# Layer 3 of a four-layer graph network: H3's three parts multiplied as one 384-column product, the decoder in written order

## The chip, the cores and the metric

The kernel runs on one core of one Trainium2 chip. The time is the device time of one execution in microseconds (us). Before the change 14 runs gave a median of 3338.72 us, with 3335.47 the lowest and 3339.78 the highest.

The core has engines that run side by side and wait for each other by semaphores: PE (matrix products, whose weight loads the profile lists as PEld), DVE (the vector engine), ACT (activation functions), POOL and SP. SP, ACT and POOL also start DMA transfers; the time that an engine's instruction queue spends on that is listed under SPq, ACTq and POOLq. Each engine runs its own instructions in order.

## What is computed

The reference takes 3125 nodes with 256 features and 100000 weighted edges through four graph layers. Each is added to its input and normalised per node. The change is in the last one. Cut to what matters (3125 nodes, 256 features in, 128 and 64 hidden):

```python
h = x @ W_conv                                # 256 -> 128
out = segment_sum(h[row] * (dis[row] * dis[col])[:, None], col) + b_conv
h = relu(out)
z = h @ W_lin + b_lin                         # 128 -> 64
d = relu(z @ W_dec1 + b_dec1)                 # 64 -> 128
out = d @ W_dec2 + b_dec2                     # 128 -> 256
x = layernorm(x + out)                        # the result
```

`dis` is one over the root of a node's degree, its own loop included. The sum over edges is a product with the (sparse) matrix of edge counts.

## The kernel before, in words

Nodes lie in 25 blocks of 128 (`NBK = 25`, `P = 128`). The matrix of edge counts is kept dense as 25 slabs, one for each block of targets: a slab is 128 x 25 x 128 numbers in bf16, 800 KB. Layer 0 builds the slabs and stores them in DRAM (`slabs`); layer 3 loads them again. `load_slab(b)` (line 728) takes one of the four buffers named `wo` and starts the load on SP (line 730). Layers 1 and 2 use the same four buffers.

The features that layer 3 sums are scaled by `dinv` and split into three bf16 parts whose sum is the f32 value. They lie in `H3`, a tile of shape [128, 25, 3, 128]: node in the block, block, part, feature. The last lines of layer 2's loop fill it, block by block (lines 1052 to 1055; the split is lines 637 to 643). So the 25th block of `H3` is there only when layer 2's last block is done.

In layer 3 the three parts are summed by `apply_parts` (line 698): for each of the 25 source blocks and each of three parts, one matmul with the slab's 128 x 128 block as weights and 128 columns of `H3`, line 702, all into one accumulator. That is 75 matmuls of 128 columns for each target block. (Layers 0 and 1 use the same line with 256 columns.)

The loop at line 1081 then does for each block b:

- line 1084, DVE: accumulator times `dinv` plus `b_conv`, into the tile `tmp`;
- line 1086, PE: transpose; line 1088, ACT: relu into `dec`;
- line 1090, PE: product with `W_lin`; line 1091, ACT: plus `b_lin`;
- line 1093, PE: product with `W_dec1`; line 1094, ACT: relu of that plus `b_dec1`;
- line 1095, PE, in the helper `product` (line 620): product with `W_dec2`, 256 columns;
- lines 1096 and 1097, DVE: added to `x2`, and `b_dec2` added;
- `norm` (line 627): DVE 629, 630, 632, ACT 633 (a square root), DVE 634 and 635;
- `write` (line 1066): four DMAs of 32 KB to the output, two started on SP and two on ACT (line 1071; block 0 uses lines 1076 and 1079).

The matmuls of lines 1086, 1090, 1093 and 620 are in f32, those of line 702 in bf16. The accumulators come from a pool `psA` of two, the results of 1090, 1093 and 620 from a pool `psM` of one.

A planner orders the instructions of each engine ahead of time, from priorities and its own costs, and may move them across the blocks of this loop and into the end of layer 2. The order that it chose is the one in the trace. Only the first stage of the kernel is inside `tc.manual_schedule` (line 500), under which the engines named get their instructions in the order in which the program writes them.

Of the kernel before, what the change touches and what calls it, by code (L numbers as in the profile page):

```python
# [8 lines left out]
F32 = mybir.dt.float32  # L9
BF = mybir.dt.bfloat16  # L10
I32 = mybir.dt.int32
AF = mybir.ActivationFunctionType
OP = mybir.AluOpType
AX = mybir.AxisListType
# [4 lines left out]
P = 128  # L19
# [12 lines left out]
def column(vec):  # L32
    return vec.rearrange("(n o) -> n o", o=1)
# [4 lines left out]
NBK = 25  # L38
# [61 lines left out]
def dense_path(ctx: ExitStack, tc: tile.TileContext, a: dict, out: bass.AP, flag: bass.AP):  # L100
    nc = tc.nc
# [22 lines left out]
    dinv = top.tile([P, NBK], F32, name="dinv")  # L124
# [7 lines left out]
    def halves(v):  # L132
        return [v[:, k * P:(k + 1) * P] for k in range(D // P)]
# [5 lines left out]
    with ExitStack() as st:  # L139
# [131 lines left out]
        for k in range(KD):  # L271
            nc.tensor.matmul(vps, attn[:, k:k + 1].to_broadcast([P, P]), we[:, k, :],
                             start=(k == 0), stop=(k == KD - 1), skip_group_check=True)
        for k in range(KD):
            nc.tensor.matmul(kps, attn[:, k:k + 1].to_broadcast([P, P]), be[:, k:k + 1],
                             start=(k == 0), stop=(k == KD - 1), skip_group_check=True)
        nc.scalar.activation(kc, kps, AF.Copy)
        for i, n in ((1, "edge_weight"), (2, "edge_weight_n2")):
            w = two.tile([P, EC], F32, name="w", bufs=1)
# [294 lines left out]
    psM = ctx.enter_context(tc.tile_pool(name="d_psM", bufs=1, space=PSUM))  # L574
    psB = ctx.enter_context(tc.tile_pool(name="d_psB", bufs=3, space=PSUM))
    psA = ctx.enter_context(tc.tile_pool(name="d_psA", bufs=2, space=PSUM))
# [25 lines left out]
    def bias(pool, v, name):  # L602
        t = pool.tile([P, v.shape[0]], F32, name=name)
        nc.scalar.dma_start(t, row_bcast(v))
        return t
# [17 lines left out]
    def project(v, w, m):  # L623
        t = transposed(halves(v))
        return product([t[:, k, :] for k in range(KD)], [w[:, k, :] for k in range(KD)], m)
# [21 lines left out]
    def halfslab(name, bufs=2, cols=P):  # L647
        t = oh.tile([P, HALF[0] * TB, P], BF, name=name, tag=name, bufs=bufs)
        return t if cols == P else t.rearrange("p t (h c) -> p (t h) c", c=cols)
# [48 lines left out]
    def apply_parts(slab, parts, m):  # L698
        p = psA.tile([P, 512], F32, name="acc")
        for s in range(NBK):  # L700
            for k in range(3):
                nc.tensor.matmul(p[:, :m], slab[:, s, :], parts[:, s, k, :m],  # L702
                                 start=(s == 0 and k == 0), stop=(s == NBK - 1 and k == 2))
        return p[:, :m]

    def apply_f32(slab, H, m):
        p = psA.tile([P, 512], F32, name="acc")
        for (o, n), t in zip(half_slabs(), slab):
            for s in range(n):
                nc.tensor.matmul(p[:, :m], t[:, s, :], H[:, o + s, :m], start=(o + s == 0), stop=(o + s == NBK - 1))  # L710
        return p[:, :m]

    def weighted_slab(pool, b, ks, kd, w3, turned=False):

        slab = []
        for o, n in half_slabs():
            os = onehot(cut(ks, b, o, n), n * TB, "os")
            od = onehot(cut(kd, b, o, n), n * TB, "od", HP)
            wo = weighted(od, [w3[:, k, o * TB:(o + n) * TB, :] for k in range(3)], n * TB)
            t = pool.tile([P, HALF[0], P], F32, name="slab_f", bufs=3)  # L720
            if turned:
                build_turned(t, n, wo, os)
            else:
                build_slab(t, b, o, n, os, wo)
            slab.append(t)
        return slab

    def load_slab(b):
        s = halfslab("wo", 4)[:, :NBK, :]
        nc.sync.dma_start(s, slabs[b].rearrange("p (s d) -> p s d", d=P))  # L730
        return s
# [20 lines left out]
    with tc.tile_pool(name="layer0", bufs=1) as pool:  # L752
        W2 = weight(pool, a["L0_gnn_W2"], "W2")
        H1 = pool.tile([P, NBK, 3, D], BF, name="H1")
        for b in range(NBK):
            load_records(b)
            slab = halfslab("wo", 4)[:, :NBK, :]
# [5 lines left out]
            p = apply_parts(slab, H0, D)  # L763
            y = wk.tile([P, D], F32, name="tmp")
            nc.scalar.activation(y, p, AF.Relu, scale=dinv[:, b:b + 1])
            p = project(y, W2, D)
# [7 lines left out]
        for j in range(TB):  # L774
            for d in range(0, NBK, 5):
                p = psT.tile([P, P], BF, name="tp")
                nc.tensor.transpose(p[:5 * NBK, :], by_tile[:, j, d * NBK:(d + 5) * NBK, 0], ident_b)
                y = pool.tile([P, P], BF, name="rowt", bufs=2)
# [27 lines left out]
        for b in range(NBK):  # L806
            p = apply_parts(load_slab(b), H1, D)
# [4 lines left out]
            p = project(x[:, b, :], WnT, D)  # L812
            nc.vector.tensor_add(H[:, b, :D], p, bn)
            m = wk.tile([P, D], F32, name="tmp")
# [25 lines left out]
    def slab_weights(b, field, by_target):  # L840

        r = wk.tile([P, TS, 4], F32, name="rec_b", bufs=3)
        v = trows if by_target else slot_rows.rearrange("(p d s j) w -> p d s (j w)", p=P, d=NBK, s=NBK)
        if by_target:
            nc.sync.dma_start(r, v[:, b * TS:(b + 1) * TS, :])
        else:
            nc.sync.dma_start(r.rearrange("p (d j) w -> p d (j w)", j=TB), v[:, :, b, :])
        w3 = wk.tile([P, 3, TS, 2], BF, name="w3")
        weights_split(w3, wk, r[:, :, field], TS, 2)
        return w3  # L850


    with tc.tile_pool(name="layer1", bufs=2) as pool:
# [39 lines left out]
        for b in range(NBK):  # L893
            w3 = wk.tile([P, 3, TS, 2], BF, name="w3")
            weights_split(w3, wk, q[:, b * TS:(b + 1) * TS], TS, 2)
            slab = weighted_slab(pool, b, keys, keyd, w3)
            p = apply_f32(slab, H, D + 1)
# [3 lines left out]
            y = wk.tile([P, D], F32, name="tmp")  # L901
# [12 lines left out]
    F0, F1 = a["L3_gnn_W_lin"].shape  # L914
    H3 = late.tile([P, NBK, 3, F0], BF, name="H3")
    with tc.tile_pool(name="layer2", bufs=1) as pool:
# [25 lines left out]
        def aggregate(b, ks, kd, w3, X, turned=False):  # L942
            return apply_f32(weighted_slab(pool, b, ks, kd, w3, turned), X, D + 1)

        with tc.tile_pool(name="layer2a", bufs=1) as pa:
# [73 lines left out]
            for b in range(NBK):  # L1019
                p = aggregate(b, keys, keyd, slab_weights(b, 1, True), x1[:, :, 1:])  # L1020
                y = pa.tile([P, D + 1], F32, name="sums", bufs=2)
# [4 lines left out]
        with tc.tile_pool(name="layer2c", bufs=1) as pb:  # L1026
            for b in range(NBK):
                p = aggregate(b, keys_t, keyd_t, slab_weights(b, 2, False), x1, True)

                y = pb.tile([P, 2 * (D + 1)], F32, name="both_in", bufs=2)  # L1030
                nc.sync.dma_start(y[:, :D + 1], a_in[:, b, :])
                nc.scalar.activation(y[:, D + 1:], p, AF.Copy)
                t = transposed(halves(y[:, :D]) + halves(y[:, D + 2:]) + halves(x[:, b, :]))
                p = psT.tile([P, 4, P], F32, name="tp")
# [3 lines left out]
                w = [m[:, k, :] for m in W_x + [W_h2h] for k in range(KD)]  # L1038
                p = product([t[:, k, :] for k in range(3 * KD)] + [r], w + [u], G)
# [3 lines left out]
                y = pb.tile([P, G], F32, name="gate")  # L1043
# [8 lines left out]
                p = project(x2[:, b, :], W_conv, F0)  # L1052
# [5 lines left out]
    with tc.tile_pool(name="layer3", bufs=1) as pool:  # L1058
        b_conv, b_dec2 = bias(pool, a["L3_gnn_b_conv"], "b_conv"), bias(pool, a["L3_gnn_b_dec2"], "b_dec2")
        w = {}  # L1060
        for n in ("W_lin", "W_dec1", "W_dec2", "b_lin", "b_dec1"):
            v = a["L3_gnn_" + n]
            v = v if n[0] == "W" else column(v)
            w[n] = pool.tile(list(v.shape), F32, name=n)
            nc.scalar.dma_start(w[n], v)
        def write(b):
            for c, p0 in enumerate((0, HP, HP + 1, 1)):
                q = (nc.sync, nc.scalar)[c % 2]
                if b:
                    n0 = FEW + NG * c + (b - 1, NG - b)[c % 2]  # L1070
                    q.dma_start(out[n0:n0 + 4 * NG * (HP // 2 - 1) + 1:4 * NG, :], x2[p0:p0 + HP - 1:2, b, :])  # L1071
                    continue
                r = range(c, FEW_ROWS, 4)
                first = c < FEW
                if first:
                    q.dma_start(out[c:c + 1, :], x2[p0:p0 + 1, b, :])
                m = len(r) - first
                n0 = P * NG + r[first]
                q.dma_start(out[n0:n0 + 4 * (m - 1) + 1:4, :], x2[p0 + 2 * first:p0 + 2 * (first + m) - 1:2, b, :])

        for b in range(NBK):
            p = apply_parts(load_slab(b), H3, F0)
            y = wk.tile([P, D], F32, name="tmp")
            nc.vector.scalar_tensor_tensor(y[:, :F0], p, dinv[:, b:b + 1], b_conv, op0=OP.mult, op1=OP.add)
            p = psT.tile([P, 4, P], F32, name="tp")
            nc.tensor.transpose(p[:, 0, :], y[:, :F0], ident)
            t = pool.tile([P, 3, P], F32, name="dec", bufs=3)
            nc.scalar.activation(t[:, 0, :], p[:, 0, :], AF.Relu)
            p = psM.tile([P, 512], F32, name="mm")
            nc.tensor.matmul(p[:F1, :P], w["W_lin"], t[:, 0, :], start=True, stop=True)  # L1090
            nc.scalar.activation(t[:F1, 1, :], p[:F1, :P], AF.Identity, bias=w["b_lin"])
            p = psM.tile([P, 512], F32, name="mm")
            nc.tensor.matmul(p[:, :P], w["W_dec1"], t[:F1, 1, :], start=True, stop=True)
            nc.scalar.activation(t[:, 2, :], p[:, :P], AF.Relu, bias=w["b_dec1"])
            p = product([t[:, 2, :]], [w["W_dec2"]], D)
            nc.vector.tensor_add(x2[:, b, :], x2[:, b, :], p)
            nc.vector.tensor_add(x2[:, b, :], x2[:, b, :], b_dec2)
            norm(b, x2)
            write(b)

# [620 lines left out]
```

## Time and profile before

The profiled execution took 3336.9 us, with a span of 3335.1 us on its core; the rest lies outside the span. It is 1.8 us under the median of the 14 runs.

| | PE | PEld | DVE | ACT | POOL |
|---|---|---|---|---|---|
| busy in the whole span, us | 2719.6 | 2100.8 | 2121.4 | 927.3 | 795.1 |
| share of the span | 82% | 63% | 64% | 28% | 24% |
| busy from 3151 to 3322 us, us | 149.9 | 123.4 | 61.3 | 29.7 | 0.0 |

Layer 3 is the last 180 us or so. Its first line 1084 starts at 3152.5 us, its last at 3319.9, and the span ends at 3335.1. In between blocks follow each other every 7.03 us. A timeline gives, for each line, the start in us, the duration in us, the engine, the line of the kernel, the operation, what is written and read, and in brackets the idle time of the engine just before, with what ended it. Neighbouring instructions of one kind are merged ("x55"). A matmul's listed duration runs to the end of its result; the next matmul can start earlier. A windows table gives, for a stretch, its length, the time for which each engine was busy in it (with the number of instructions) and the granted PE clock, 1.00 being full speed.

### The profile page before, as it was taken

Reading aid. Unit: us, or ns where it says so; the run is one execution under the profiler, and the core shown is the slowest. Engines: PE = TensorE matmul, PEld = TensorE weight load, DVE = VectorE, ACT = ScalarE, POOL = GpSimd, SP = SyncE. Lnnn points to the kernel's source line nnn. Section 1 sums busy time; section 2 is a strip of 40 time slices with the busy share of each in tenths; the row PEclk is TensorE's granted clock in tenths of the full one; section 3 lists DMA queues with packets and bytes.
Section 4 is the critical chain, followed back from the end, with each engine's and each line's share of the span. In section 5 each row is a group of like instructions: output and inputs, shape, how many; then the busy total and the mean of one; then the engine's idle time right before and its main releaser. Section 6 shows DMA issues by size and latency. Waiting matters only on the chain.

```text
span 3335.1 us, 66141 instructions
## 1 busy us (share of the span) xinstructions
PE 2719.6 (82%) x28824; PEld 2100.8 (63%) x28824; DVE 2121.4 (64%) x3844; ACT 927.3 (28%) x1844; POOL 795.1 (24%) x879
## 2 busy tenths in 40 slices
PE   4466654555541999999899999999999999999987
PEld 2234432333221888788688888888887676676676
DVE  8999964555542655355588888667666566566333
ACT  2222222222220444200122222222223343343311
POOL 4677777777775000000000000000000000000000
PEclk7556555555555999999899999999999999999999
DMA  4122222222212211556300000100011101100242
GB/s 146 52 65 79 79 67 69 70 69 70 77 30 77 88 70 80 194 215 228 129 2 2 2 2 14 36 16 16 16 14 16 12 10 10 12 10 7 75 133 88
DMA packets 169936, 203.86 MB, mean 61 GB/s; under 512 B 117592, under 2 KB 142669, under 8 KB 163363
## 3 DMA queue, kind: packets, MB, share of 16 engines
q1 hardware_dynamic: 130955, 186.94, 17.2%
q10 hardware_dynamic: 13592, 10.94, 1.1%
q0 software_dynamic: 25088, 1.66, 0.7%
q8 instruction: 227, 3.72, 0.5%
q14 instruction: 74, 0.61, 0.1%
HBM read 167.60 MB, written 31.86 MB: 60 GB/s over the span
## 4 chain that ended last, share of the span: by engine, by line
PE 47%; POOL 20%; DVE 17%; issue 8%; ACT 4%; DMA 2%; ACTq 1%; POOLq 0%; DVEq 0%; SPq 0%
POOL table L473 19%; PE acc L710 17%; PE acc L702 12%; PE mm L620 7%; PE slab L682 5%; DVE wo L836 4%; DVE os L656 3%; PE tp L613 2%; PE slab L694 1%; PE look L798 1%; ACT xT L614 1%; DVE st L629 1%; DVE od L656 1%; DMA rec_b<-table 1%; ACTq L1071 1%
## 5 line engine op out<-in xcount | busy, mean ns | idle before, releaser
L473 POOL DMA_INDIRECT table<-rec,row x784 | 755.5, 964 | 275.9 <-issue 228.9
L710 PE MATMUL acc<-x,slab_f 128*128 128x257 f32 x2500 | 592.6, 386 | 0.0
L836 DVE TENSOR_TENSOR wo<-od,w 128x1664 bf16<-128x1664 bf16 (+1 forms) x450 | 434.3, 984 | 132.0 <-PE slab L682 108.2
L702 PEld LDWEIGHTS <-wo 128*128 128x128 bf16 x5625 | 476.0, 99 | 61.9 <-issue 10.7
L710 PEld LDWEIGHTS acc<-x,slab_f 128*128 128x128 f32 x2500 | 455.9, 189 | 71.4 <-issue 5.7
L682 PEld LDWEIGHTS <-os 128*128 128x128 bf16 x8750 | 297.5, 99 | 116.6 <-issue 91.9
L702 PE MATMUL acc<-H,wo 128*128 128x256 bf16 (+1 forms) x3750 | 342.5, 247 | 1.2 <-ACT H L639 0.8
L656 DVE TENSOR_TENSOR os<-iota_b,keys 128x3328 bf16<-128x3328 bf16 (+1 forms) x150 | 272.8, 1818 | 111.1 <-PE slab L682 110.0
L391 PEld LDWEIGHTS <-ohd 128*52 128x52 bf16 x784 | 106.6, 159 | 338.3 <-issue 299.8
L710 PE MATMUL acc<-features,slab_f 128*128 128x257 f32 x1250 | 297.3, 388 | 0.0
L682 PE MATMUL slab<-wo,os 128*128 128x64 bf16 x7500 | 261.1, 193 | 13.6 <-ACT slab_f L683 8.4
L710 PEld LDWEIGHTS acc<-features,slab_f 128*128 128x128 f32 x1250 | 227.9, 190 | 43.3 <-issue 12.1
L388 PE MATMUL cnt<-pre,ident_b 52*52 52x442 bf16 x48 | 25.1, 523 | 276.6 <-ACT pre L398 276.6
L683 ACT ACTIVATE slab_f<-slab 128x512 f32<-128x512 f32 (+1 forms) x350 | 182.6, 549 | 145.9 <-PE slab L682 140.8
L702 PE MATMUL acc<-features,wo 128*128 128x256 bf16 x1875 | 212.7, 273 | 0.0
L965 POOL COPY keys_t<-keys 128x2500 bf16<-128x2500 bf16 x1 | 2.5, 2522 | 721.6 <-ACT tmp L902 721.6
L319 DVE TENSOR_TENSOR aside<-aside,features 128x256 f32<-128x256 f32 x25 | 10.8, 432 | 223.9 <-ACT features L316 223.9
L391 PE MATMUL cnt<-oh,ohd 128*52 128x416 bf16 (+15 forms) x784 | 152.1, 383 | 1.3 <-DVE ohd L331 1.3
L485 ACT ACTIVATE tick<-gap 1x1 f32<-1x1 f32 x47 | 7.4, 158 | 516.6 <-POOL tock L486 378.1
L656 DVE TENSOR_TENSOR od<-iota_b,keyd 128x1664 bf16<-128x1664 bf16 (+1 forms) x150 | 147.5, 983 | 0.0
L437 DVE TENSOR_SCALAR eq<-gap 128x512 bf16<-128x512 f32 x196 | 121.8, 680 | 29.4 <-ACT tick L485 29.2
L1044 DVE TENSOR_TENSOR gate<-mm,bx 128x512 f32<-128x512 f32 x25 | 17.3, 692 | 190.9 <-PE mm L620 190.9
(293 smaller groups left out, 3701.9 us busy)
## 6 DMA issues: line engine op xcount, KB each, us to landing
ea<-in_edge_attr SPq DMA_DIRECT2D x49, 1024.0 KB
wo<-slabs SPq DMA_DIRECT2D x50, 800.0 KB
os<-rows SPq DMA_DIRECT2D x25, 832.0 KB
slabs<-wo SPq DMA_DIRECT2D x25, 800.0 KB
od<-rows SPq DMA_DIRECT2D x25, 768.0 KB
table<-rec,row POOLq DMA_INDIRECT x784
dr<-db_row SPq DMA_DIRECT2D x49, 208.0 KB
rec_b<-table SPq DMA_DIRECT2D x75, 100.0 KB
```

The costliest lines, as they stand in the source:

```text
L391: nc.tensor.matmul(cnt[:, c + 1:, :], it["by_target"][:, c], it["by_source"][:, c:c + 1, :].to_broadcast([P, CH - c, KB]), start=False, st ...
L437: nc.vector.tensor_scalar(eq[:, 4 * g:4 * g + 4, :], gap, 0.0, None, op0=OP.is_equal)
L473: i = nc.gpsimd.indirect_dma_start(out=table, out_offset=bass.IndirectOffsetOnAxis(ap=ready[k][:, c:c + 1], axis=0), in_=rec[:, k * CH + c ...
L613: nc.tensor.transpose(p[:, j, :], srcs[i + j], ident)
L614: nc.scalar.activation(t[:, i:i + n, :], p[:, :n, :], AF.Copy)
L620: nc.tensor.matmul(p[:, :m], l, r, start=(i == 0), stop=(i == len(w) - 1))
L656: nc.vector.tensor_tensor(in_pairs(t[:, :n, :]), repeat(iota_b[:, :cols], n), pair(k, cols), op=OP.is_equal)
L682: nc.tensor.matmul(p[:, i - g, own], l, r, start=(m == 0), stop=(m == len(terms) - 1))
L683: nc.scalar.activation(dst[:, g:g + w, :], p[:, :w, :], AF.Copy)
L702: nc.tensor.matmul(p[:, :m], slab[:, s, :], parts[:, s, k, :m], start=(s == 0 and k == 0), stop=(s == NBK - 1 and k == 2))
L710: nc.tensor.matmul(p[:, :m], t[:, s, :], H[:, o + s, :m], start=(o + s == 0), stop=(o + s == NBK - 1))
L836: nc.vector.tensor_tensor(in_pairs(t[:, :n, :]), in_pairs(oh[:, :n, :]), pair(w3[k], HP), op=OP.mult)
```

## The change

`apply_parts` is no longer used by layer 3. For each block b and each source block s there is one matmul of 384 columns (`H3[:, s]` with parts and features side by side) in place of three of 128; the accumulator holds the three partial sums side by side. A new DVE instruction adds the three (`tensor_reduce` over a view in which the parts are innermost, 128 x 384 in, 128 x 128 out, into the unused half of the tile `tmp`), and line 1084's operation then reads that half.

The 25 matmuls of a block are cut into five pieces of five. The decoder of a block is cut into five steps, and the steps of block b-1 stand between the pieces of block b: step, piece, step, piece and so on. The results of the `W_lin` and `W_dec1` products move from the pool `psM` to the pool `psB` (three buffers, tag `slab`). Slabs are loaded three blocks ahead, and the whole is written inside `tc.manual_schedule` for PE, DVE, ACT and SP.

```diff
-        for b in range(NBK):
-            p = apply_parts(load_slab(b), H3, F0)
+        slab, acc = {}, {}
+
+        def piece(b, i):
+            for s in range(5 * i, 5 * i + 5):
+                nc.tensor.matmul(acc[b][:, :3 * F0], slab[b][:, s, :], H3[:, s].rearrange("p k m -> p (k m)"),
+                                 start=(s == 0), stop=(s == NBK - 1))
+
+        def decode(b):
             y = wk.tile([P, D], F32, name="tmp")
-            nc.vector.scalar_tensor_tensor(y[:, :F0], p, dinv[:, b:b + 1], b_conv, op0=OP.mult, op1=OP.add)
+            nc.vector.tensor_reduce(y[:, F0:], acc.pop(b)[:, :3 * F0].rearrange("p (k m) -> p m k", k=3), axis=AX.X, op=OP.add)
+            nc.vector.scalar_tensor_tensor(y[:, :F0], y[:, F0:], dinv[:, b:b + 1], b_conv, op0=OP.mult, op1=OP.add)
+            yield
             p = psT.tile([P, 4, P], F32, name="tp")
             nc.tensor.transpose(p[:, 0, :], y[:, :F0], ident)
             t = pool.tile([P, 3, P], F32, name="dec", bufs=3)
             nc.scalar.activation(t[:, 0, :], p[:, 0, :], AF.Relu)
-            p = psM.tile([P, 512], F32, name="mm")
-            nc.tensor.matmul(p[:F1, :P], w["W_lin"], t[:, 0, :], start=True, stop=True)
-            nc.scalar.activation(t[:F1, 1, :], p[:F1, :P], AF.Identity, bias=w["b_lin"])
-            p = psM.tile([P, 512], F32, name="mm")
-            nc.tensor.matmul(p[:, :P], w["W_dec1"], t[:F1, 1, :], start=True, stop=True)
-            nc.scalar.activation(t[:, 2, :], p[:, :P], AF.Relu, bias=w["b_dec1"])
+            yield
+            p = psB.tile([P, 4, P], F32, name="slab")
+            nc.tensor.matmul(p[:F1, 0, :], w["W_lin"], t[:, 0, :], start=True, stop=True)
+            nc.scalar.activation(t[:F1, 1, :], p[:F1, 0, :], AF.Identity, bias=w["b_lin"])
+            yield
+            p = psB.tile([P, 4, P], F32, name="slab")
+            nc.tensor.matmul(p[:, 0, :], w["W_dec1"], t[:F1, 1, :], start=True, stop=True)
+            nc.scalar.activation(t[:, 2, :], p[:, 0, :], AF.Relu, bias=w["b_dec1"])
+            yield
             p = product([t[:, 2, :]], [w["W_dec2"]], D)
             nc.vector.tensor_add(x2[:, b, :], x2[:, b, :], p)
             nc.vector.tensor_add(x2[:, b, :], x2[:, b, :], b_dec2)
             norm(b, x2)
             write(b)
 
+        with tc.manual_schedule(engines={e.engine for e in (nc.tensor, nc.vector, nc.scalar, nc.sync)}):
+            for b in range(3):
+                slab[b] = load_slab(b)
+            for b in range(NBK + 1):
+                steps = decode(b - 1) if b else iter(())
+                if b < NBK:
+                    acc[b] = psA.tile([P, 512], F32, name="acc")
+                if b + 3 < NBK:
+                    slab[b + 3] = load_slab(b + 3)
+                for i in range(5):
+                    next(steps, None)
+                    if b < NBK:
+                        piece(b, i)
```

## The prediction, made before the changed kernel was run

> **What bounds the kernel now.** The page comes first: its span, and the rows of the 40 slices for PE and the PE clock.
>
> ```profile
> span 3335.1 us, 66141 instructions
> PE   4466654555541999999899999999999999999987
> PEclk7556555555555999999899999999999999999999
> ```
>
> Layer 3 fills the last two slices. PE looks full there, but busy shares are averages, so next comes the timeline of one block from the middle of layer 3, cut to what matters.
>
> ```profile
> 3190.39 0.42 DVE L1096 TENSOR_TENSOR features<-features,mm 128x256 f32<-128x256 f32 x1 [4.14 <-PE mm L620]
> ...
> 3192.60 0.41 DVE L635 TENSOR_SCALAR features<-features,stats,rstd 128x256 f32<-128x256 f32 x1
> 3193.01 0.35 DVE L1084 SCALAR_TENSOR_TENSOR tmp<-acc,dinv,b_conv 128x128 f32<-128x128 f32 x1
> ...
> 3193.05 1.38 ACTq L1071 DMA_DIRECT2D out<-features  x2
> ...
> 3193.42 0.33 PE L1086 MATMUL tp<-ident,tmp 128*128 128x128 f32 x1
> ...
> 3193.58 0.50 PE L702 MATMUL acc<-H,wo 128*128 128x128 bf16 x6
> ...
> 3194.53 0.28 ACT L1088 ACTIVATE dec<-tp 128x128 f32<-128x128 f32 x1 [2.15 <-PE acc L702]
> ...
> 3194.86 0.43 PE L1090 MATMUL mm<-dec,W_lin 128*64 128x128 f32 x2 [0.77 <-ACT dec L1088]
> ...
> 3195.74 0.48 PE L1093 MATMUL mm<-dec,W_dec 64*128 64x128 f32 x2
> ...
> 3196.68 0.70 PE L620 MATMUL mm<-W_dec,dec 128*128 128x256 f32 x2
> ...
> 3197.22 3.23 PE L702 MATMUL acc<-H,wo 128*128 128x128 bf16 x55
> 3197.42 0.42 DVE L1096 TENSOR_TENSOR features<-features,mm 128x256 f32<-128x256 f32 x1 [4.06 <-PE mm L620]
> ```
>
> Read it as a ring. From line 1096 to the end of 635, DVE normalises block b: 2.62 us. Straight behind that, with no idle time, it starts line 1084 of block b+1 (0.35), then PE transposes. ACT can't take the transposed block (1088) before 4.14 after 1096, since its queue is busy for 1.38 us with the two output DMAs of block b, which wait for 635. Then W_lin at 4.47, W_dec1 at 5.35, W_dec2 at 6.29, and line 1096 of block b+1 at 7.03. So a chain through DVE, ACT and PE sets the pace, not PE's amount of work. The planner fits the 75 sums into its gaps: 6, 7, 7 and 55, the 55 beside the normalisation; PE idles only 0.77 us a block.
>
> The last view is the granted clock. It changes at 3153.02, 3159.85 and 3323.70: distances of 6.83 and 163.85 us, 2 and 48 times 3.41. So I cut windows of 3.41 us that end where the clock fell (first, second, third and fifth; the fourth and sixth are those where it stayed).
>
> ```profile
> 3149.61:3153.02 3.41, 1.66 (x11) 1.06 (x12) 1.12 (x4) 1.06 (x4) 0.00 (x0) 1.00 0.00 0
> 3320.28:3323.70 3.42, 1.36 (x6) 0.73 (x7) 0.00 (x0) 1.01 (x3) 0.00 (x0) 1.00 0.16 38
> 1074.30:1077.70 3.40, 1.19 (x22) 1.00 (x20) 0.00 (x0) 0.00 (x0) 0.00 (x0) 1.00 0.84 194
> 1371.30:1374.70 3.40, 2.30 (x21) 1.96 (x19) 1.59 (x6) 0.48 (x2) 0.00 (x0) 1.00 0.75 243
> 1374.70:1378.10 3.40, 0.98 (x8) 0.64 (x7) 0.00 (x0) 0.28 (x1) 0.00 (x0) 1.00 0.95 384
> 3187.00:3190.40 3.40, 2.58 (x24) 1.88 (x25) 0.01 (x1) 1.01 (x3) 0.00 (x0) 1.00 0.74 216
> ```
>
> The second number is PE's busy time. With 49% or less the clock fell to 0.50; with 67 and 76% it held.
>
> **The change, part by part.** Times count from line 1096 of block b-1.
>
> *Sums.* 55 matmuls of 128 columns in 3.23 us are (3.23 - 0.22)/54 = 55.7 ns apart. For 256 columns, layer 1 has 50 in 5.62 us, (5.62 - 0.27)/49 = 109.2. One step of 128 costs 53.5, so 384 columns cost 162.7 ns (bounds: 109, and three times 55.7 = 167). A block needs 4.07 us in place of 4.18: 0.11 less, on an engine that doesn't set the pace. A piece of five is 0.81. What matters is where pieces stand. In written order each is in PE's queue ahead of the next step.
>
> *Added reduce.* 128x384 from PSUM. The SBUF row of line 816 (256 in, 0.42 us) and the PSUM row of 801 (150 in, 0.31) give 0.155 + 1.04 ns an element: 0.56. Bounds: 0.42 (as 816), and 0.83 if the stride costs what it does in line 560, 784 strided elements in 1.53 us, 1.75 ns each. I take 0.56, as PSUM row 801 is nearest. In written order it stands behind the normalisation of block b-1 on DVE (`write` and `norm` end step five, the reduce opens the next block): 2.62 to 3.18. Line 1084's operation then runs 3.21 to 3.56 (0.35 kept; its operand is now in SBUF), transpose at 3.62 against 3.03.
>
> *ACT.* The two output DMAs keep their place; ACT is free at 4.14 as before. The transposed block is there at 4.0. So of the 0.59 that the reduce adds, ACT's queue hides nearly all: W_lin could start at 4.47 still. SP's queue has each load written before the writes of the block before; a load waits for a buffer freed an iteration ago and a write for 635, so a later load is held one block at most, and each is issued three blocks (23 us) ahead, when a whole block moves 928 KB in 7.03 us at a DMA share of 0.45: nothing. The `psB` move costs nothing: three free buffers and no builder left.
>
> *Pieces in the chain.* After the transpose (PE takes 0.16 until the next matmul starts: 3193.42 to 3193.58) a piece runs 3.78 to 4.60, so W_lin starts at 4.60. It occupies 0.36 (start to start), W_dec1 0.42, W_dec2 0.54. Now W_lin to W_dec1 is 0.36 + 0.82 = 1.18 against 0.88 before, W_dec1 to W_dec2 0.42 + 0.81 = 1.23 against 0.94. W_dec1 at 5.78, W_dec2 at 7.01, and line 1096 after 0.74 more: **7.75 us a block against 7.03**. Lower bound with the cheap reduce: 7.62; upper: 8.02.
>
> *What goes late.* PE has pieces until 1.43 after 1096 (the last of a block and the first of the next, from -0.20 on), then nothing until the transpose at 3.62: a stall of 2.19 us in every block, where before 47 sums stood. A 3.41 us window that holds it whole has 1.22 busy, 36%: the clock falls. Going by 49%, any window with 1.74 us of the stall falls. Each block slides against the windows, and walking through it (7.75 us is 2.27 windows, 9.4 is 2.75) a window falls in some 15 of 24 blocks. For 3.41 us PE then runs at half speed, in the part of the block that is all PE, so about 1.7 us of work is late; less what lies in the stall, 1.65. After line 1084's start at 3152.5 the clock stayed low for two windows, 6.83 us, which would cost 3.3; other rises (1067.5, 1384.9) took one dense window. I take one, as the pieces are dense.
>
> Here a page speaks against me. The Trainium skill, "TensorE: Matmul & The Clock Gate", section "Why this matters for your kernels", asks only for no idle gaps over some 3 us between bursts. By it 2.19 us would be harmless, and the sum below would lose its clock term and be 3360. This trace disagrees: in the window that ends at 3153.02 no single gap exceeds 1 us, and the clock fell.
>
> *Head and tail.* Before, the ends of layer 2 hid the sums of two blocks, and line 1096 ran 3158.17 to 3317.29 for blocks 0 to 23: 159.1 us, 2.6 under 23 rings. In written order only block 0 can run ahead. New: 23 x 7.75 = 178.3, **+19.2**. The head: block 0's last matmul still waits for H3's last part (3152.18), the reduce adds 0.56 and the clock is low there as before: +1.3 by 1096 of block 0. If block 0's 24 matmuls (3.9 us) can't start before layer 2's last product at 3150.4, another 2.1; I take half, **+2.3** in all. The last block (7.49 from 1096 to 1096) has no pieces, but waits for ACT as before: 4.14 + 3.35 = 7.49: 0. The end after 1096 stays.
>
> *Sum.* 19.2 + 2.3 + 15 x 1.65 = 46. The profiled execution took 3336.9, giving 3383; the median is 1.8 higher: **3385**.
>
> **Rivals.**
> *No clock drops.* The bracket of 49 to 67% counts listed durations, and short f32 products may count less than dense pieces do. Then 3338.7 + 21.5 = 3360. For: steady blocks before held 1.00 throughout; against: the four falls.
> *Long drops.* Two windows each: 21.5 + 15 x 3.3 = 71, 3410. For: 3153 to 3159.85, in this very decoder; against: other rises.
> *Faster.* If the order written lets reduce, 1084's operation and 1088 of the next block stand ahead of `norm` and `write`, PE sets the pace: 5 x 0.81 + 0.16 + 0.36 + 0.42 + 0.54 = 5.55 us, 23 x 5.55 = 128, 31 less: with the head 3310. For: the decoder then hides wholly behind pieces; against: the diff writes `norm` first, and ACT's DMAs too. It decides from a ring under 6.9 us, 0.85 off DVE's and ACT's part alike.
> *The change does next to nothing.* If pieces cost less in the chain than worked out (0.59 of the 0.72) and the clock holds, a ring of about 7.1: 3338.7 + 4 + 2 = 3345.
>
> **How the numbers follow.** Clock drops of one window 0.57 (3368 to 3402: 10 to 20 blocks, reduce and head bounds), no drops 0.20 (3352 to 3367), long drops 0.10, faster 0.08, next to nothing 0.05. The range 3352 to 3408 holds the first two and some of the long drops, 0.8. Within 0.2% (6.7 us, about what this kernel's runs can tell): the last, 0.05. Slower 0.87, faster 0.08.
>
> **What would show it.** In the changed trace: line 620's helper to the next line 1096 unchanged at 0.74; between 1096 and the next, 7.7 us where the clock is 1.00 and about 9.4 where it falls; PE idle 2.2 us before the transpose, ended by DVE; a reduce of 0.56; five-matmul runs of 0.81 plus latency; a granted clock of about 0.8 over layer 3, with steps 3.41 us apart. I am wrong if DVE runs the reduce ahead of line 629, if the stall is under 1.2 us, or if the clock stays at 1.00.

## The result and the profile after

The changed kernel takes 3376.9 us, median of 6 runs (3375.25 to 3378.63), against 3338.54 before (28 runs). That is 38.4 us more, a ratio of 1.0116 with a 95% interval of 1.0106 to 1.0126. The profiled execution took 3377.3 us with a span of 3375.5.

The line that adds the product with `W_dec2` (1096 before, 1109 now) is a good clock for the stage. From its first to its last start layer 3 took 166.6 us before (3158.17 to 3324.78) and takes 205.2 us now (3159.99 to 3365.22): 38.6 of the 40.4 us between the two profiled executions; the other 1.8 us lie ahead of it. Below, "layer 3" means this stretch.

First the page of the changed kernel: the span, and the slices of PE and of the PE clock.

```profile
span 3375.5 us, 63667 instructions
PE   4467645545532999999799999999999999999776
PEclk7555655555556999999899999999999999999888
```

The last three slices hold layer 3. PE is at 7, 7 and 6 tenths where it was at 8 and 7, and its clock at 8. Next the timeline of two neighbouring blocks: start, duration, engine, line, operation, what is written and read, and the idle time just before with what ended it.

```profile
3249.63 0.55 DVE L1092 TENSOR_REDUCE tmp<-acc 128x128 f32<-128x384 f32 x1
3249.74 1.38 ACTq L1071 DMA_DIRECT2D out<-features  x2
3250.22 0.35 DVE L1093 SCALAR_TENSOR_TENSOR tmp<-tmp,dinv,b_conv 128x128 f32<-128x128 f32 x1
...
3250.62 0.33 PE L1096 MATMUL tp<-ident,tmp 128*128 128x128 f32 x1 [1.95 <-DVE tmp L1093]
...
3251.22 0.28 ACT L1098 ACTIVATE dec<-tp 128x128 f32<-128x128 f32 x1 [2.15 <-PE tp L1096]
...
3251.69 0.43 PE L1101 MATMUL slab<-dec,W_lin 128*64 128x128 f32 x2
...
3252.97 0.48 PE L1105 MATMUL slab<-dec,W_dec 64*128 64x128 f32 x2
...
3254.21 0.59 PE L620 MATMUL mm<-W_dec,dec 128*128 128x256 f32 x2
...
3254.84 0.42 DVE L1109 TENSOR_TENSOR features<-features,mm 128x256 f32<-128x256 f32 x1 [4.28 <-PE mm L620]
...
3257.06 0.41 DVE L635 TENSOR_SCALAR features<-features,stats,rstd 128x256 f32<-128x256 f32 x1
...
3258.38 0.33 PE L1096 MATMUL tp<-ident,tmp 128*128 128x128 f32 x1 [1.95 <-DVE tmp L1093]
...
3259.45 0.44 PE L1101 MATMUL slab<-dec,W_lin 128*64 128x128 f32 x2
...
3261.53 0.79 PE L1105 MATMUL slab<-dec,W_dec 64*128 64x128 f32 x2
...
3263.51 0.59 PE L620 MATMUL mm<-W_dec,dec 128*128 128x256 f32 x2
...
3264.14 0.42 DVE L1109 TENSOR_TENSOR features<-features,mm 128x256 f32<-128x256 f32 x1 [5.82 <-PE mm L620]
```

The ring is closed in the written order. Normalisation of a block (up to line 635), then reduce and line 1093 of the next on DVE, and PE stands idle for 1.95 us before each transpose. W_lin waits for the piece in front of it (3251.69), then the two other steps follow behind their pieces. The first block shown lasts to 3254.84, 7.75 us after its predecessor; the second takes 9.30 us. What makes it longer is between W_lin and W_dec2, 4.06 us in place of 2.52, and there a piece of five took nearly twice its time (1.78 us, with its end, against 0.99). The windows table of the same stretch shows why (length, PE busy time and number of instructions, granted clock, then DMA):

```profile
3256.33:3259.75 3.42, 1.47 (x9) 1.00 0.15 38
3259.75:3263.16 3.41, 3.41 (x12) 0.50 0.76 241
3263.16:3266.57 3.41, 2.57 (x15) 1.00 0.00 0
3266.57:3269.99 3.42, 2.31 (x13) 1.00 0.40 74
3269.99:3273.40 3.41, 3.41 (x20) 1.00 0.51 205
3273.40:3276.81 3.41, 1.46 (x9) 1.00 0.15 38
```

A window that held the whole gap had PE busy for 1.47 us, and the next one ran at half clock. Two windows that held half of a gap each (2.57 and 2.31) left the clock alone. Five windows later it happens again: a long and a short block, 9.30 + 7.76 = 17.06 us, are just five windows (5 x 3.413 = 17.07), so the pattern locks. From the second step to the 22nd every second one is long.

Of the 24 steps from block to block, 12 are made longer by a fall of the clock (a 13th fall, at 3362.15 us, comes in the last block, which has no pieces). The difference in layer 3 comes out as: 24 steps of 7.76 are 186.2 us, 19.6 over before; 12 falls at 1.54 us are 18.5; single steps of 7.87 to 9.46 make up the rest, 0.5.

### The profile page after: what moved, and what is told of

Read it like the earlier page. It is cut to its first block, busy times and chain, and to the rows that moved or that the text cites. A ratio compares the mean times of both kernels' runs of the same rounds, so it can differ in the third digit from the quotient of the medians.

```text
span 3375.5 us, 63667 instructions
## 1 busy us (share of the span) xinstructions
PE 2728.1 (81%) x27574; PEld 2055.5 (61%) x27574; DVE 2133.6 (63%) x3869; ACT 927.4 (27%) x1844; POOL 795.1 (24%) x879
## 4 chain that ended last, share of the span: by engine, by line
PE 49%; POOL 19%; DVE 17%; issue 8%; ACT 4%; DMA 2%; ACTq 0%; POOLq 0%; DVEq 0%; SPq 0%
POOL table L473 19%; PE acc L710 17%; PE acc L702 11%; PE mm L620 7%; PE slab L682 5%; DVE wo L836 4%; DVE os L656 3%; PE acc L1087 2%; PE tp L613 2%; PE slab L694 1%; PE look L798 1%; ACT xT L614 1%; DVE st L629 1%; DMA table<-rec,row 1%; DVE od L656 1%
## 5 line engine op out<-in xcount | busy, mean ns | idle before, releaser
L702 PEld LDWEIGHTS <-wo 128*128 128x128 bf16 x3750 | 363.4, 98 | 48.1 <-issue 3.8
L682 PE MATMUL slab<-wo,os 128*128 128x64 bf16 x7500 | 261.1, 193 | 13.6 <-ACT slab_f L683 8.4
L702 PE MATMUL acc<-H,wo 128*128 128x256 bf16 x1875 | 218.8, 273 | 0.0
```

The costliest lines, as they stand in the source:

```text
L682: nc.tensor.matmul(p[:, i - g, own], l, r, start=(m == 0), stop=(m == len(terms) - 1))
```

## The experiments

All later runs were on other chips, on which the first stage of every kernel took over 200 us longer; layer 3 was the same there (the changed kernel again: 205.3 us, with the same 12 falls). So each is told with its difference to the kernel before on its own chip and by layer 3. "Step" is the time from one start of the `W_dec2` addition to the next.

| run | step at full clock, us | falls in 24 steps | layer 3, us |
|---|---|---|---|
| before | 7.03 | 0 | 166.6 |
| changed | 7.76 | 12 | 205.2 |
| changed, 11 idle products | 7.76 | 0 | 187.4 |
| changed, 3 idle products | 7.76 | 0 | 187.1 |
| changed, 1 idle product | 7.76 | 9 | 201.0 |
| changed, pieces moved | 7.11 | 0 | 172.3 |
| changed, no reduce | 7.62 | 3 after the start | 191.6 |
| changed, no reduce, no DMA on ACT | 7.17 | 0 | 172.3 |
| written order alone | 7.73 | 5 | 194.6 |
| wide product alone | 5.99 in the mean | 0 | 143.8 |
| late normalisation | 5.59 | 0 | 132.6 |
| late normalisation, narrow | 5.78 | 0 | 136.4 |
| late normalisation, early output | 10.6 with falls | nearly all | 258.1 |

**The clock: PE's gap filled with products that nobody reads.** The edit, with 11 in the first run, then 3 and 1:

```diff
                     if b < NBK:
                         piece(b, i)
+                    if 0 < b < NBK and i == 0:
+                        idle = psL.tile([P, 512], F32, name="look")
+                        for s in range(11):
+                            nc.tensor.matmul(idle[:, :3 * F0], slab[b][:, s, :], H3[:, s].rearrange("p k m -> p (k m)"),
+                                             start=True, stop=True)
```

> The changed kernel, with 11 products of 384 columns that nobody reads put between the first piece of a block and the transpose, where PE stood idle for 1.95 us; 11 x 0.163 = 1.79 us, so they should end before the transpose can start. It does more work than the changed kernel and computes the same. If the clock drops are the stall's doing: no drop in the ring, every block 7.76 us as in the blocks at full clock, 12 x 1.54 = 18.5 us less than 3376.9, so 3358. Rival, that the long blocks of 9.3 us come from something else (late slabs, the output writes): unchanged, 3377, or a little more for the added work.

Measured: 1.0064 times before (1.0047 to 1.0081), 23 us slower than before. No falls, every step but the odd one 7.76 to 7.77, layer 3 at 187.4 us: 17.8 us less than the changed kernel for more work. The long steps were the clock's.

> The changed kernel with 3 products that nobody reads, in place of 11, in PE's stall. In the changed kernel the windows of 3.41 us before a fall held 1.39 to 1.53 us of PE busy time; the run without the reduce fell at 1.68 and held at 1.74. Three products add 0.49: 1.88 at the least, over half of a window (1.71). If half a window is the rule, no falls in the ring: 24 blocks of 7.76 to 7.9, 187 us. Rival, that the length of the longest gap decides (1.95 us falls to 1.5, over the 1.36 us that held): falls as before, 205.

> As before with one such product: 0.16 more, 1.55 to 1.69 us, still under half of a window. If half a window is the rule, the clock falls as in the changed kernel, in about 12 of 24 blocks, and layer 3 takes about 205 us. Rival, that any break of the idle gap keeps the clock up: 187.

Each was measured once, 23.5 and 35.7 us slower than before. Three products were enough: 187.1 us, no fall in the ring. One was not: 9 falls, 201.0 us. The windows with the least PE time in these two runs (first the run with three, then two stretches of the run with one):

```profile
3553.32:3556.73 3.41, 1.88 (x12) 1.00 0.29 57
```

```profile
3504.28:3507.69 3.41, 1.63 (x10) 1.00 0.12 30
3507.69:3511.11 3.42, 3.42 (x11) 0.50 0.73 248
3572.55:3575.96 3.41, 1.63 (x11) 1.00 0.12 28
3575.96:3579.37 3.41, 3.41 (x20) 1.00 0.04 10
```

So it goes by about the share of a window, not by one long gap: with three products a gap of 1.46 us was left and the clock held, while the run without the reduce (below) had falls with no gap over 1.35 us. But half a window of listed PE time is no exact border: at 1.63 us the clock fell in one window and held in another. The run with the written order alone fell at 1.75, the one without the reduce held at 1.74. The widest exceptions lie in the last block of two runs told below, the one with the pieces moved (first two lines, held at 1.42 although PE then stood idle for 2.60 us on end) and the late normalisation with narrow products (fell at 1.86):

```profile
3542.08:3545.50 3.42, 1.42 (x8) 1.00 0.00 0
3545.50:3548.91 3.41, 1.29 (x6) 1.00 0.16 39
```

```profile
3538.67:3542.08 3.41, 1.86 (x7) 1.00 0.00 0
3542.08:3545.49 3.41, 0.00 (x0) 0.50 0.18 43
```

In layer 3 of all 14 profiles, a window at full clock with up to 1.40 us of listed PE time was always followed by a fall, one with 1.88 us or more never; in between both happened. The border doesn't carry over to other products: in an earlier stage of the kernel before, the clock fell after a window with 3.14 us (473.56 to 476.97). A listed duration includes the wait for the result (one product of 384 columns is listed with 0.33 us and occupies 0.16), differently for each kind of product, so the sum of durations is only near what the clock's control counts. What it counts stays open.

**The pieces between the steps.** The same 25 products, cut otherwise:

```diff
+        CUTS = (0, 10, 13, 16, 19, 25)
-            for s in range(5 * i, 5 * i + 5):
+            for s in range(CUTS[i], CUTS[i + 1]):
```

> The changed kernel with the same 25 products cut as 10, 3, 3, 3 and 6 in place of five times 5: fewer between the decoder's steps, more before the transpose. Theory of the ring: three products take 0.49 us, less than the wait for ACT, so the 0.55 us that pieces put into the ring are gone; W_lin starts 4.47 after the block's first addition, as ACT's queue allows, and the ring is back at 7.03 us: 0.73 x 24 = 17.5 us less. PE's stall falls from 1.95 to about 1.2 us, and all idle time of a block (1.4 us) still lies close together, so a window has 58% busy, between what fell (49%) and what held (67%): with no drops 3377 - 18.5 - 17.5 = 3341, with a drop in half of the blocks about 3355. Rival, that the reduce on DVE sets the ring: 3377 less at most the clock part, 3358.

Measured: 1.0025 times before (1.0015 to 1.0036), 8.8 us slower; steps of 7.11 us, layer 3 172.3. That is 33 us less than the changed kernel, with reduce and order of engines untouched. 0.65 us a step came back from pieces that no longer stand in the ring (7.03 was expected, 7.11 came), and there were no falls: the least busy window had 2.0 us, but for the one in the last block shown above.

**The reduce.** Line 1093's operation reads the first third of the accumulator directly:

```diff
-            nc.vector.tensor_reduce(y[:, F0:], acc.pop(b)[:, :3 * F0].rearrange("p (k m) -> p m k", k=3), axis=AX.X, op=OP.add)
-            nc.vector.scalar_tensor_tensor(y[:, :F0], y[:, F0:], dinv[:, b:b + 1], b_conv, op0=OP.mult, op1=OP.add)
+            nc.vector.scalar_tensor_tensor(y[:, :F0], acc.pop(b)[:, :F0], dinv[:, b:b + 1], b_conv, op0=OP.mult, op1=OP.add)
```

> The changed kernel without the reduce: line 1093's operation reads the first third of the accumulator, so the second and third parts of H3 are multiplied but left out of the sum. My account: the transpose comes 0.59 us earlier, but ACT's queue is held by the output DMAs until 4.14 us after the first addition, so W_lin starts at 4.47 in place of 4.60: the ring only falls from 7.76 to about 7.62, and PE's idle time, now in two parts (1.4 and 0.5 us), still makes the clock fall in about half of the blocks: 3377 - 0.14 x 24 = 3374, or 3365 to 3374 if there are a few drops less. Rival, that the reduce is what makes the ring longer: 0.59 x 24 = 14 us less, 3363, or 3344 if the drops go with it.

Measured: 1.0080 times before (1.0063 to 1.0097). The step fell to 7.62, as worked out: 0.14 us for an instruction of 0.55. The falls I had wrong: 3 after the first blocks in place of 12, so layer 3 took 191.6 us, 13.6 less than in the changed kernel. By the time alone the rival would fit (14 us less); the step of 7.62 is what speaks against it. PE's gap was 1.35 us and the second, before W_lin, 0.39, and the least busy windows came to lie at 1.67 us, where the clock fell, and from 1.74 us up, where it held.

The second half of that claim is that ACT's queue stands ready to bound the same place. Without the reduce, and with `q = nc.sync` for all four output DMAs of a block:

> The changed kernel without the reduce (parts two and three of H3 are multiplied but left out of the sum) and with all four output DMAs of a block started on SP, none on ACT. Theory: the reduce and ACT's queue bound the same step side by side, so each alone gives little (without the reduce 7.62 us at full clock), both together give what the pieces leave: transpose at 3.03 after the first addition, W_lin at 4.00 behind its piece, 7.14 us a block at full clock. Rival, that ACT's queue was not what held W_lin: 7.62 again. If SP's queue now holds the slab loads: above 7.6.

Measured once: 9.9 us slower than before, steps of 7.17 us, no falls. With output started on ACT (first lines, the run without the reduce) the relu comes when the two DMAs are started, 1.19 us after the transpose began; with none there (second lines) it comes after 0.43 us:

```profile
3446.76 1.38 ACTq L1071 DMA_DIRECT2D out<-features  x2
...
3447.05 0.33 PE L1095 MATMUL tp<-ident,tmp 128*128 128x128 f32 x1 [1.35 <-DVE tmp L1092]
...
3448.24 0.28 ACT L1097 ACTIVATE dec<-tp 128x128 f32<-128x128 f32 x1 [2.15 <-PE acc L1087]
```

```profile
3441.99 0.33 PE L1095 MATMUL tp<-ident,tmp 128*128 128x128 f32 x1 [1.36 <-DVE tmp L1092]
...
3442.42 0.28 ACT L1097 ACTIVATE dec<-tp 128x128 f32<-128x128 f32 x1 [1.39 <-PE tp L1095]
```

Taking away the reduce gave 0.14 us a step; with ACT's two DMAs gone as well it is 0.59. (ACT's part alone wasn't tried.)

**The two parts of the change, each alone.** Written order with three narrow products:

```diff
-                nc.tensor.matmul(acc[b][:, :3 * F0], slab[b][:, s, :], H3[:, s].rearrange("p k m -> p (k m)"),
-                                 start=(s == 0), stop=(s == NBK - 1))
+                for k in range(3):
+                    nc.tensor.matmul(acc[b][:, :F0], slab[b][:, s, :], H3[:, s, k, :],
+                                     start=(s == 0 and k == 0), stop=(s == NBK - 1 and k == 2))
```

with the reduce left out as above, since the three parts now add up in one sum.

> The other part alone: written order, steps and pieces as in the changed kernel, but three products of 128 columns for each source block, so 15 products to a piece, all into one sum, and no reduce. Theory: a piece takes 15 x 55.7 = 0.84 us, W_lin starts at 4.47 as ACT's queue allows, and the ring is 4.47 + 0.36 + 0.84 + 0.42 + 0.84 + 0.74 = 7.66 us, 0.63 over before; PE's busy time in a window comes near one half, so some windows fall, 4 to 12 of them at 1.55 us: layer 3 takes 185 to 196 us, 18 to 29 more than before. Rival, that the order is harmless and the reduce is to blame: about as before, 167.

Measured: 1.0093 times before (1.0076 to 1.0110). Steps of 7.73, 5 falls, layer 3 194.6 us: 28 us lost in layer 3 without any wide product. On the same chip the changed kernel came to 1.0106 (1.0089 to 1.0123), as expected here:

> The changed kernel unaltered, so that it stands beside its variants on one chip. Layer 3 alone is compared, from the first to the last start of the line that adds the product with W_dec2 (166.6 us before the change, 205.2 after): 205 again, with a block of about 9.3 us wherever the clock falls and 7.76 elsewhere.

The wide product and the reduce in the planner's loop:

```diff
         for b in range(NBK):
-            p = apply_parts(load_slab(b), H3, F0)
+            slab, acc = load_slab(b), psA.tile([P, 512], F32, name="acc")
+            for s in range(NBK):
+                nc.tensor.matmul(acc[:, :3 * F0], slab[:, s, :], H3[:, s].rearrange("p k m -> p (k m)"),
+                                 start=(s == 0), stop=(s == NBK - 1))
             y = wk.tile([P, D], F32, name="tmp")
-            nc.vector.scalar_tensor_tensor(y[:, :F0], p, dinv[:, b:b + 1], b_conv, op0=OP.mult, op1=OP.add)
+            nc.vector.tensor_reduce(y[:, F0:], acc[:, :3 * F0].rearrange("p (k m) -> p m k", k=3), axis=AX.X, op=OP.add)
+            nc.vector.scalar_tensor_tensor(y[:, :F0], y[:, F0:], dinv[:, b:b + 1], b_conv, op0=OP.mult, op1=OP.add)
```

> One part alone: the 25 products of 384 columns and the reduce in the loop of the kernel before, in the planner's order. Theory: the reduce adds 0.59 us on DVE, but ACT's queue hides 0.56 of it, and the planner puts few products between the decoder's steps, so the ring grows from 7.03 to between 7.1 and 7.4 us, no clock drops: 2 to 9 us slower than before. Rival, that the reduce counts in full: 7.6 us a block, 14 us slower. Second rival, that the wide products alone bring the change's loss: 38 us slower.

Measured: 0.9935 times before (0.9918 to 0.9951), 22.7 us **faster**. The ring and the sign were expected wrongly; only that the clock would not fall came true. Steps run from 3.2 to 7.4 us, 5.99 in the mean. DVE's timeline shows it:

```profile
3470.19 0.42 DVE L1100 TENSOR_TENSOR features<-features,mm 128x256 f32<-128x256 f32 x1 [4.47 <-PE mm L620]
3470.65 0.42 DVE L1101 TENSOR_TENSOR features<-features,b_dec 128x256 f32<-128x256 f32 x1
...
3470.99 0.55 DVE L1087 TENSOR_REDUCE tmp<-acc 128x128 f32<-128x384 f32 x1
3471.46 0.42 DVE L629 BATCH_NORM_STATS2 st<-features 128x6 f32<-128x256 f32 x1
3471.79 0.33 DVE L1088 SCALAR_TENSOR_TENSOR tmp<-tmp,dinv,b_conv 128x128 f32<-128x128 f32 x1
```

The planner put the reduce and line 1088's operation of the next block ahead of and into the normalisation (lines 629 to 635), so blocks overlap and the ring is open: from 3400 us on PE is listed busy for 136.4 of 144 us, where before the change it was 145.7 of layer 3's 166.6. I had kept the order of the kernel before. Why its plan differs so much with the new operations isn't visible in a trace of the chip.

**The ring cut open in written order.** The last additions and the normalisation of block b move behind the reduce and scaling of block b+1 on DVE, the square root behind W_lin's activation on ACT, the output behind W_dec1's. `late` is the generator of the block before; its steps are called after those of the newer block.

```diff
+        CUTS = (0, 8, 12, 16, 20, 25)
...
             p = product([t[:, 2, :]], [w["W_dec2"]], D)
+            yield
             nc.vector.tensor_add(x2[:, b, :], x2[:, b, :], p)
             nc.vector.tensor_add(x2[:, b, :], x2[:, b, :], b_dec2)
-            norm(b, x2)
+            st = wk.tile([P, 6], F32, name="st")
+            nc.vector.bn_stats(st, x2[:, b, :])
+            nc.vector.bn_aggr(stats[:, b, :], st)
+            r = rstd[:, b:b + 1]
+            nc.vector.tensor_scalar(r, stats[:, b, 1:2], EPS, None, op0=OP.add)
+            yield
+            yield
+            nc.scalar.activation(r, r, AF.Sqrt)
+            nc.vector.reciprocal(r, r)
+            nc.vector.tensor_scalar(x2[:, b, :], x2[:, b, :], stats[:, b, 0:1], r, op0=OP.subtract, op1=OP.mult)
+            yield
             write(b)
...
+            steps = iter(())
-            for b in range(NBK + 1):
-                steps = decode(b - 1) if b else iter(())
+            for b in range(NBK + 2):
+                late, steps = steps, decode(b - 1) if 0 < b <= NBK else iter(())
...
                     next(steps, None)
+                    next(late, None)
```

> The changed kernel with block b's last additions, normalisation and output moved behind the first step of block b+1 on DVE, its square root behind W_lin's activation of block b+1 on ACT and the output DMAs behind W_dec1's; pieces cut as 8, 4, 4, 4 and 5. Theory: the ring through DVE and ACT is cut, and PE's own work sets the pace, 25 x 0.163 + 1.48 = 5.55 us, no drops in the clock; 23 x 5.55 = 128 against 159 before, less 31, plus about 2 for the head: 3310. Rival, that slab loads (928 KB a block, 166 GB/s needed against 132 in the kernel before) or PE's switching take over: 6.0 to 6.5 us a block, 3320 to 3333. If the normalisation was not what held the ring: 3358 or more.

Measured: 0.9913 times before (0.9896 to 0.9930), 31.1 us faster, the best of all. Each step takes 5.59 or 5.60 us. The windows table of 115 us in layer 3 (length, then busy time of PE, PEld, DVE, ACT and POOL, clock, DMA) shows that PE is now the bound, at full clock:

```profile
3400.00:3515.00 115.00, 113.53 (x649) 64.66 (x647) 62.11 (x185) 22.27 (x81) 0.00 (x0) 1.00 0.47 146
```

With ACT's part of that undone (the three added bare `yield`s before the square root and before `write` left out), DVE's order alone is mended:

> The variant with the late normalisation, but only DVE's order is mended: reduce and scaling of block b+1 stand ahead of block b's last additions, while ACT's square root and output DMAs of block b still stand ahead of the relu of block b+1. Theory: ACT's queue alone then closes the ring: normalisation 2.62, DMAs 1.52, relu to W_lin 0.33, steps and pieces 0.36 + 0.65 + 0.42 + 0.65 + 0.54, the piece after it and the reduce and scaling of the next block 0.82 + 1.15: about 9.1 us a block at full clock and more where the clock falls, slower than the changed kernel's average of 8.55. Rival, that DVE's order was all that mattered: 5.6 to 6.0.

Measured once: 98.5 us slower than before. But for the last, steps are 10.5 to 12.3 us, above the 9.1 expected, since the clock now falls in nearly every one. The pieces are those of the run before, so cutting them anew isn't what opened the ring. ACT's queue closes it by itself:

```profile
3506.68 0.41 DVE L1120 TENSOR_SCALAR features<-features,stats,rstd 128x256 f32<-128x256 f32 x1
...
3507.12 1.38 ACTq L1071 DMA_DIRECT2D out<-features  x2
3508.60 0.28 ACT L1099 ACTIVATE dec<-tp 128x128 f32<-128x128 f32 x1 [2.15 <-issue]
...
3508.93 0.69 PE L1102 MATMUL slab<-dec,W_lin 128*64 128x128 f32 x2 [3.30 <-ACT dec L1099]
```

The transpose had run at 3504.70. The relu that reads it stood behind a square root and two DMAs of an older block until 3508.60, 3.6 us after the transpose's end.

Last, the late normalisation with narrow products and no reduce, which prices the wide product where PE sets the pace:

> The variant with the late normalisation (5.59 us a block), but with three products of 128 columns for each source block and no reduce. There PE's own work sets the pace, so this prices the wide product: 75 x 55.7 in place of 25 x 162.7 ns is 0.11 us a block, so 5.70 us a block, 135 us for the 24 blocks against 132.6. If DVE's reduce counted there, it would be faster than 5.59; if the many weight loads cost more than the middle of layer 3 before showed (59 ns a product at the dearest), up to 5.9.

Measured: 0.9927 times before (0.9911 to 0.9944); 5.78 us a step, so the wide product is worth 0.19 us a step where 0.11 was worked out: 3.8 us over layer 3.

## Why the prediction held, point by point

3385 was predicted, 3376.9 measured; +46 against the profiled execution before, +40.4 measured between the two spans. These are 19.4 for 23 rings (19.2 predicted), 18.9 for the falls and some odd steps (25), 1.8 ahead of the first addition (2.3) and 0.4 for the last block (0). The ring came out as worked out; what was too large is the clock's term.

- *The ring.* 7.75 us a step predicted, 7.76 measured. Each moment of it came within 0.1 us: the reduce 0.55 (0.56), the transpose 3.5 us after the first addition (3.62), ACT's relu 4.1 (4.14), W_lin 4.6 (4.60). That pieces in the ring and not the reduce make it longer was shown by moving the pieces (7.11) and by taking the reduce away (7.62).
- *ACT's queue.* That it hides nearly all of the reduce was shown by the two runs without it: 0.14 us for the reduce while ACT starts the output, another 0.45 once ACT doesn't.
- *PE's gap.* 2.19 us predicted, 1.95 listed. My figure began where the next product could have started; the profile counts the last product to the end of its result, 0.16 later, and the transpose came 0.08 earlier. That 47 sums stood in this stretch before is a slip: from 1.43 on it was some 29. The sum doesn't use it.
- *The clock.* The mechanism was shown by the fillers. The term was too large: 15 falls at 1.65 us, 25 in all; 12 at 1.54, 18.5 measured. Both factors were a little off. The walk of blocks against windows that I did by hand missed that long and short blocks together are five windows, which pins the falls to every second block. The bracket of 49 to 67% came from six chosen windows. For layer 3's products it closed to near half, but the listed durations don't give it exactly, and with other products falls came far above it. The sign given, a granted clock of about 0.8 over layer 3, was off: it is 0.89, and the 15 falls predicted would have made 0.88.
- *Head and tail.* +2.3 predicted. The first addition came 1.8 us later, of which 1.05 was there already in layer 2 (line 1032 of the last block at 3134.74 against 3133.69): 0.8 for the head. Block 0's products did run ahead into the end of layer 2, so the half of 2.1 was not owed. The last block cost 0.4, not 0.
- *The rule on idle gaps.* The Trainium skill ("TensorE: Matmul & The Clock Gate", section "Why this matters for your kernels") asks for no idle gaps over some 3 us, by which the clock's term would be nothing and the sum 3360. Gaps of 1.95 us cost 18 us here. The measurement decides.
- *The rival that was faster.* It named its condition: reduce and scaling on DVE and relu on ACT ahead of the older block's normalisation and output. It gave 29 us less than before; the run that made the condition true gave 31.1 less, and the one that made only DVE's half true gave 98.5 more.

What the prediction didn't ask is what the wide product does in the planner's hands. It called it 0.11 us on an engine that doesn't set the pace. Alone it brings 22.7 us. Some 4 us of that may be the cheaper products (3.8 between the two late runs); the rest goes with the planner's other order, which no run tried with narrow products. The written order then threw all of it away and 38 us more.

## What to carry to other kernels

A written order freezes every queue, so draw the ring before writing it: from each instruction back to what stands ahead of it on its own engine, DMA starts included. Here one misplaced normalisation and two DMA starts cost more than any arithmetic, and moving them, with the pieces cut anew, was worth 70 us between two orders of the same instructions. Pieces of bulk work between dependent steps should be no longer than the wait that they cover; put the rest where the engine really idles. And a regular PE gap of 2 us in every 8 may be charged twice, once as a wait and once as a slower clock after it: three useless products of 0.16 us each saved 18 us of layer 3.

## What was not expected of the hardware

The clock's windows are 3.413 us apart and stay in step, from 3153 to 3324 us before the change and from 3164 to 3362 after it. So a loop can lock to them: with steps of 7.76 and 9.30 us the sum is five windows. In layer 3 a window with PE listed busy for well under half its time (up to 1.40 us) was always followed by one at half clock; around half it went either way.

In the steady blocks of the changed kernel one dense window brought the clock back every time. At the start of layer 3 it stayed low for two, after the change (first two lines) and before it (last two):

```profile
3150.52:3153.94 3.42, 1.63 (x8) 0.50 0.00 0
3153.94:3157.35 3.41, 3.41 (x12) 0.50 0.73 245
```

```profile
3153.03:3156.44 3.41, 3.41 (x21) 0.50 0.83 296
3156.44:3159.86 3.42, 3.42 (x23) 0.50 0.47 189
```

After the change the first of the two was not dense, so again one dense window was enough. Before it, a window listed as busy throughout left the clock low, and why isn't known.
